# A recurrent recommendation kernel: the GRU gate matmuls split into four matmuls of 32 output columns

## The chip, the cores and the metric

The kernel runs on one core of one Trainium2 chip. The metric is the device time of one launch in microseconds (us). The kernel before takes 2076.75 us, the median of three runs between 2075.74 and 2077.31.

A core has a matrix engine (TensorE, "PE" in the profile, its weight loads apart as "PEld"), a vector engine (VectorE, "DVE"), an engine for activation functions (ScalarE, "ACT"), GpSimd ("POOL") and SyncE ("SP"), which here only issues DMAs. Each works through its own queue in order. TensorE reads SBUF and writes PSUM[...].

## The reference

For 1024 users there is a history of T = 100 item embeddings of 128 numbers. A GRU runs over the history, its states are the keys of an attention, and a second recurrence runs over the keys. All of it is f32.

```python
def gru_step(h, x_t):
    gi = x_t @ gru_Wih.T + gru_bih
    gh = h @ gru_Whh.T + gru_bhh
    i_r, i_z, i_n = jnp.split(gi, 3, axis=-1)
    h_r, h_z, h_n = jnp.split(gh, 3, axis=-1)
    r = jax.nn.sigmoid(i_r + h_r)
    z = jax.nn.sigmoid(i_z + h_z)
    n = jnp.tanh(i_n + r * h_n)
    h_new = (1.0 - z) * n + z * h
    return (h_new, h_new)
...
feat = jnp.concatenate([keys, q, keys - q, q * keys], axis=-1)
score = _mlp(feat, [(att_W0, att_b0), (att_W1, att_b1), (att_W2, att_b2)], relu)   # 512 -> 80 -> 40 -> 1
score = jnp.where(mask[:, :, None] == 1, score, -jnp.inf)
attn = jax.nn.softmax(score, axis=1)[..., 0]
pooled = jnp.einsum('bt,btd->bd', attn, keys)
```

After that, an AUGRU (a GRU whose update gate is scaled by a weight taken from `pooled`) runs over the keys, the state at each user's length is taken, and a small MLP (640 -> 200 -> 80 -> 1, sigmoid) gives one score per user.

## The kernel before, in words

Features lie on the 128 partitions, users along the free dimension. The 1024 users are two halves of HB = 512, so that a matrix product of a half is a 128 x 512 matmul and fills one PSUM bank.

The kernel has two stages. The first (`gru_phase`) runs the GRU, the attention MLP, a softmax that is kept up to date in blocks of steps, and the weighted sum of the keys ("pooled"). The second (`augru_phase`) runs the AUGRU with users sorted by length, so that its matmuls get narrower, from 510 columns to 96, and the last MLP.

The order of the instructions is written out by hand: each engine executes what concerns it in the order of the Python program. One step `s` of the loop at line 823 issues on TensorE:

- for half 0 and then half 1, the gates (`Half.gru`, line 497): r from x and h (two matmuls that accumulate in one bank), h's part of n and x's part of n (one matmul each, in banks of their own), z from x and h (two matmuls). That is six 128 x 128 x 512 matmuls for a half, twelve for a step, all issued at line 507. The pool `ps` gives their banks: six in turn.
- the attention MLP of step `s - 1` (`attend`, line 660). Its layers have 80, 40 and 1 outputs. They are packed into blocks of R = 32 outputs, and three time steps are worked on together: layer one of step s - 1, layer two of the step before, layer three of the one before that. A block is one matmul at line 669 of 32 output columns that writes 32 partitions of a bank, at the array's column position of these partitions. There are sixteen of them in a step, in four turns of four, one for each column position, into two banks of the pool `pa`.

The rest of a step lies on other engines. ScalarE takes the sigmoids and the tanh (lines 519, 538, 539) and the relu of the attention (line 708). VectorE does the GRU's elementwise work (lines 527, 537, 542 to 544), the 32 x 32 transposes of the new state (line 556), the sum of the attention result and the item's share (line 703, "f") and the product of state and item for the next attention (line 582). `stage()` puts parts of a block's softmax between the halves' work in the steps that follow a block's end; `scores` (lines 755 and 759) uses a bank of `pa` for a moment, which the attention's second result of that step needs next. GpSimd adds up the masked history (lines 493, 494) and the weighted keys (lines 605, 606). SyncE loads x and the mask two steps ahead and writes keys and scores to HBM.

Between the stages comes a tail (lines 887 to 954): the last attention turns, the last softmax blocks, a layer of the final MLP that doesn't depend on the AUGRU (line 636), and the rest of the weighted sum; then `pooled` goes through HBM to the second stage.

The wih and whh tiles hold the three gates' weights as [128, 3, 128], so that `w[:, g, :]` is a gate's 128 x 128 weight. The gate matmul is

```python
nc.tensor.matmul(
    p,
    lhsT=w[:, g, :],
    rhs=v,
    start=(j == 0),
    stop=(j == len(parts) - 1),
)
```

and the attention's is

```python
s = ts(q, R)
nc.tensor.matmul(p[i][s, :], lhsT=w[:, s], rhs=v, start=start, stop=stop)
```

In the built program every matmul carries the size of the array tile that it uses: 128 x 128 for the gates, for the item's share (line 245, once) and for the whole second stage, 128 x 32 for the attention.

## Time and profile before

| What | Value |
|---|---|
| median of the three runs | 2076.75 us |
| span of the profiled execution, first to last instruction | 2049.3 us |
| median less span | 27.4 us |
| granted TensorE clock, mean | 0.996 |
| TensorE busy | 2021.1 us, 99% |
| VectorE busy | 1756.6 us, 86% |
| GpSimd busy | 1305.1 us, 64% |
| ScalarE busy | 826.3 us, 40% |
| gate matmuls (L507), records | 1200 of x and 1188 of h |
| attention matmuls (L669), records | 3216 |
| instructions | 26686 |

The profiled execution has no time of its own beside its span; a run's time holds what lies ahead of the first and after the last instruction too.

The profile page gives the busy time of each engine, the chain of waits that ended last with its shares by line, and groups of instructions (line, engine, operation, output<-inputs, shape, count, busy time and mean duration, idle time before them and who ended it). The timeline gives single instructions or merged runs of them in order of time: start, duration, engine, line, count, and in brackets the idle time before. An f32 matmul shows as two weight loads and two matmuls. Matmuls overlap, and their ends are modelled: the distance of starts tells more than their durations. The table of windows gives each engine's busy time in a stretch. Line numbers are those of the kernel before; in the changed kernel everything below the change lies one line further down.

### The profile page before, as it was taken

How to read it: one execution, taken by the hardware profiler on the slowest of the kernel's cores; microseconds unless marked ns; L12 is line 12 of the kernel's file. 1: busy time of each engine (PE TensorE's matmuls, PEld its weight loads, DVE VectorE, ACT ScalarE, POOL GpSimd, SP SyncE). 2: the span in 40 equal slices, each digit the busy share in tenths (PEclk: the TensorE clock that was granted, in tenths of full speed). 3: DMA queues.
4: the chain of work that ended last, by engine and by line, in shares of the span. 5: the costliest groups of instructions: out<-in, count | busy, mean ns of one | idle time of the engine just before them, and what ended most of it. 6: DMA issues, size and time to landing. Idle time of an engine off the chain costs nothing.

```text
span 2049.3 us, 26686 instructions
## 1 busy us (share of the span) xinstructions
PE 2021.1 (99%) x8288; PEld 975.3 (48%) x8288; DVE 1756.6 (86%) x3066; ACT 826.3 (40%) x1508; POOL 1305.1 (64%) x1291
## 2 busy tenths in 40 slices
PE   8999999999999999999999999999899999999998
PEld 3343333333333333333333333334444556678997
DVE  6888999998989988888889898999587777888986
ACT  3334343343434343433434333434344444444554
POOL 0233939659796959597796958899753354443431
PEclk9999999999999999999999999999999999999999
DMA  4452333223334334332343233231542333333432
GB/s 118 98 115 89 104 95 105 79 85 109 112 97 114 115 98 126 108 101 84 98 124 104 91 103 104 89 104 55 169 121 87 95 111 95 94 101 93 88 80 38
DMA packets 241587, 204.73 MB, mean 100 GB/s; under 512 B 59270, under 2 KB 204394, under 8 KB 241434
## 3 DMA queue, kind: packets, MB, share of 16 engines
q1 hardware_dynamic: 227498, 170.43, 29.9%
q0 software_dynamic: 12352, 32.31, 5.7%
q8 instruction: 67, 1.10, 0.2%
q14 instruction: 86, 0.70, 0.1%
q10 hardware_dynamic: 1584, 0.20, 0.1%
HBM read 146.82 MB, written 54.40 MB: 98 GB/s over the span
## 4 chain that ended last, share of the span: by engine, by line
PE 89%; DVE 4%; DMA 2%; POOL 2%; issue 1%; ACT 1%; SPq 0%; DVEq 0%; ACTq 0%; POOLq 0%
PE ps L507 46%; PE pm L669 16%; PE ph L1075 5%; PE pr L1075 4%; PE pu L1075 4%; PE ph L1071 4%; PE pu L1071 4%; PE pr L1071 4%; DMA rows<-keys_d,idx_k 1%; DVE kq L582 1%; POOL pooled L606 1%; POOL kw L605 1%; DMA x<-in_hist_x 0%; DVE ps L537 0%; DVE d L543 0%
## 5 line engine op out<-in xcount | busy, mean ns | idle before, releaser
L507 PE MATMUL ps<-x,wih 128*128 128x512 f32 x1200 | 592.6, 603 | 4.2 <-DMA x<-in_hist_x 4.2
L507 PE MATMUL ps<-hn,whh 128*128 128x512 f32 x1188 | 574.4, 592 | 0.0
L507 PEld LDWEIGHTS ps<-x,wih 128*128 128x128 f32 x1200 | 220.9, 191 | 327.7 <-issue 252.7
L507 PEld LDWEIGHTS ps<-hn,whh 128*128 128x128 f32 x1188 | 225.7, 190 | 284.1 <-issue 275.8
L493 POOL TENSOR_TENSOR xm<-x,m 128x512 f32<-128x512 f32 x200 | 247.3, 1237 | 137.4 <-DMA m<-mask_d 137.1
L538 ACT ACTIVATE ps<-ps,bih 128x512 f32<-128x512 f32 x200 | 132.4, 662 | 484.7 <-DVE ps L537 484.7
L519 ACT ACTIVATE r<-ps,brz 128x512 f32<-128x512 f32 x200 | 137.5, 688 | 375.1 <-PE ps L507 373.9
L494 POOL TENSOR_TENSOR hist<-hist,xm 128x512 f32<-128x512 f32 x200 | 266.5, 1333 | 15.7
L174 POOL DMA_INDIRECT rows<-keys_d,idx_k x220 | 214.0, 973 | 84.9 <-POOL rows L173 70.8
L606 POOL TENSOR_TENSOR pooled<-pooled,kw 128x512 f32<-128x512 f32 x191 | 254.5, 1333 | 15.0
L605 POOL TENSOR_TENSOR kw<-kt,e 128x512 f32<-128x512 f32 x191 | 219.3, 1148 | 64.7 <-DVE e L778 64.6
L582 DVE TENSOR_TENSOR kq<-hn,item 128x512 f32<-128x512 f32 x200 | 228.3, 1181 | 0.0
L669 PE MATMUL pm<-hn,wk 128*32 128x512 f32 x1200 | 211.8, 596 | 3.3 <-ACT q L248 1.7
L669 PE MATMUL pm<-kq,wkq 128*32 128x512 f32 x1200 | 209.4, 592 | 0.0
L1083 ACT ACTIVATE c<-ph,bh 128x96 f32<-128x96 f32 (+41 forms) x198 | 96.5, 488 | 275.5 <-PE ph L1075 275.5
L669 PE MATMUL pm<-mv,w 128*32 128x512 f32 (+1 forms) x808 | 196.2, 598 | 0.9 <-DVE e L759 0.9
L703 DVE TENSOR_TENSOR f<-pm,q 128x512 f32<-128x512 f32 x200 | 128.4, 684 | 50.9 <-PE pm L669 50.7
L542 DVE TENSOR_TENSOR d<-hn,ps 128x512 f32<-128x512 f32 x198 | 136.1, 687 | 34.9 <-ACT ps L538 32.6
L543 DVE TENSOR_TENSOR d<-ps,d 128x512 f32<-128x512 f32 x200 | 138.4, 692 | 23.8 <-ACT ps L539 6.3
L537 DVE TENSOR_TENSOR ps<-ps,u 128x512 f32<-128x512 f32 x200 | 140.0, 700 | 21.2 <-PE ps L507 0.5
L173 POOL COPY rows<-rest 128x1 f32<-128x1 f32 x188 | 35.4, 188 | 191.5 <-DVE rest L1112 190.1
L527 DVE SCALAR_TENSOR_TENSOR u<-ps,bhh,r 128x512 f32<-128x512 f32 x198 | 146.9, 742 | 11.6 <-PE ps L507 11.2
(180 smaller groups left out, 2943.9 us busy)
## 6 DMA issues: line engine op xcount, KB each, us to landing
x<-in_hist_x SPq DMA_DIRECT2D x212, 256.0 KB
keys_d<-kt SPq DMA_DIRECT2D x48, 1024.0 KB
m<-mask_d SPq DMA_DIRECT2D x200, 128.0 KB
rows<-keys_d,idx_k POOLq DMA_INDIRECT x220, 3.0
s_b<-mv SPq DMA_DIRECT2D x200, 8.0 KB
keys_d<-kt SPq DMA_DIRECT2D x32, 64.0 KB
at<-att_d SPq DMA_DIRECT2D x34, 48.0 KB
mask_i<-in_mask SPq DMA_DIRECT2D x8, 200.0 KB
```

The lines of the kernel that those rows point to most:

```text
L174: nc.gpsimd.indirect_dma_start(out=r[:, at, :], out_offset=None, in_=keys_d[q], in_offset=bass.IndirectOffsetOnAxis(ap=idx_k[:, k, i : i + ...
L493: nc.gpsimd.tensor_mul(d, x, m)
L494: nc.gpsimd.tensor_add(acc, acc, d)
L507: nc.tensor.matmul(p, lhsT=w[:, g, :], rhs=v, start=(j == 0), stop=(j == len(parts) - 1),)
L527: nc.vector.scalar_tensor_tensor(out=u, in0=ph, scalar=bhh[:, 2:3], in1=r, op0=ALU.add, op1=ALU.mult,)
L537: nc.vector.tensor_add(pi, pi, u)
L582: nc.vector.tensor_mul(kq, h, item[:, self.cols])
L605: eng.tensor_mul(d, k, w)
L606: eng.tensor_add(acc, acc, d)
L669: nc.tensor.matmul(p[i][s, :], lhsT=w[:, s], rhs=v, start=start, stop=stop)
L1071: nc.tensor.matmul(p, lhsT=m[:, 1, :], rhs=k, start=True, stop=False)
L1075: nc.tensor.matmul(p, lhsT=m[:, 0, :], rhs=v, start=False, stop=True)
```

## The change

In `Half.gru`, the helper `gate` issues four matmuls where it issued one. Each takes 32 of the 128 columns of the gate's weight and writes the 32 partitions of the bank that belong to them. The moving operand (x or h, 128 x 512) is the same for the four. R is 32 and P is 128. Both parts of a gate accumulate as before, quarter by quarter.

```diff
                 def gate(g, parts):
                     p = ps.tile([P, HB], F32, tag="g", name=f"ps{g}")
                     for j, (w, v) in enumerate(parts):
-                        nc.tensor.matmul(
-                            p,
-                            lhsT=w[:, g, :],
-                            rhs=v,
-                            start=(j == 0),
-                            stop=(j == len(parts) - 1),
-                        )
+                        for q in range(P // R):
+                            nc.tensor.matmul(
+                                p[ts(q, R), :],
+                                lhsT=w[:, g, ts(q, R)],
+                                rhs=v,
+                                start=(j == 0),
+                                stop=(j == len(parts) - 1),
+                            )
                     return p
```

In the built program the gate matmuls of the changed kernel are 4776 with a tile of 128 x 32, where they were 1194 with 128 x 128. Nothing else differs but the semaphore waits and values that follow from the count.

## The prediction

> **What bounds the kernel now.** I read the page first: busy shares, the chain that ended last, the costliest groups.

> ```profile
> PE 2021.1 (99%) x8288; PEld 975.3 (48%) x8288; DVE 1756.6 (86%) x3066; ACT 826.3 (40%) x1508; POOL 1305.1 (64%) x1291
> ...
> PE ps L507 46%; PE pm L669 16%; PE ph L1075 5%; PE pr L1075 4%; PE pu L1075 4%; PE ph L1071 4%; PE pu L1071 4%; PE pr L1071 4%; DMA rows<-keys_d,idx_k 1%; DVE kq L582 1%; POOL pooled L606 1%; POOL kw L605 1%; DMA x<-in_hist_x 0%; DVE ps L537 0%; DVE d L543 0%
> ...
> L507 PE MATMUL ps<-x,wih 128*128 128x512 f32 x1200 | 592.6, 603 | 4.2 <-DMA x<-in_hist_x 4.2
> L507 PE MATMUL ps<-hn,whh 128*128 128x512 f32 x1188 | 574.4, 592 | 0.0
> ```

> The chain is TensorE for 46% + 16% of the span in the two lines of the first stage: gates (L507) and attention MLP (L669). An f32 matmul leaves two weight loads and two matmul records, so 1194 gate matmuls are 2388 records. TensorE practically never idles there. But a modelled busy time hides small gaps, so next comes its own timeline, one step of the loop (start, duration, line, count).

> ```profile
> 703.62 1.02 PE L507 MATMUL ps<-hn,whh 128*128 128x512 f32 x2
> 704.57 0.62 PE L669 MATMUL pm<-hn,wk 128*32 128x512 f32 x2
> ...
> 705.02 0.60 PE L669 MATMUL pm<-hn,wk 128*32 128x512 f32 x2
> ...
> 705.45 0.60 PE L669 MATMUL pm<-kq,wkq 128*32 128x512 f32 x2
> ...
> 707.17 1.04 PE L669 MATMUL pm<-kq,wkq 128*32 128x512 f32 x8
> 708.14 1.13 PE L507 MATMUL ps<-x,wih 128*128 128x512 f32 x2
> 709.10 1.88 PE L507 MATMUL ps<-hn,whh 128*128 128x512 f32 x4
> 710.82 1.88 PE L507 MATMUL ps<-x,wih 128*128 128x512 f32 x4
> ```

> Read the starts. The next attention starts at 718.64, so a step is 718.64 - 704.57 = 14.07 us; 93 of the 97 complete steps from 30.3 to 1399.3 us have exactly this length. Gate records follow each other every 1.72 / 4 = 0.43 us (0.4295 over a longer run). Attention records come four at a time, one per 32-column tile, and a group of four takes the same 0.43 (705.02 to 705.45). A step has 24 gate records and 32 / 4 = 8 groups: 32 slots x 0.4295 = 13.74 us. The remaining 0.33 us lies at the two changes of shape: the attention starts 0.09 late (703.62 + 0.86 = 704.48) and its first slot is 0.02 long; the gates start 0.11 late (707.17 + 0.86 = 708.03), and their first two slots take 0.96, 0.10 too many. The weight loads show the reason for the uneven parts:

> ```profile
> 704.57 0.11 PEld L669 LDWEIGHTS pm<-hn,wk 128*32 128x32 f32 x2 [0.76 <-PE ps L507]
> ...
> 708.14 0.30 PEld L507 LDWEIGHTS ps<-x,wih 128*128 128x128 f32 x2 [0.84 <-DVE hn L544]
> 708.67 0.19 PEld L507 LDWEIGHTS ps<-hn,whh 128*128 128x128 f32 x1 [0.24 <-issue]
> ```

> Inside a run, the load for the next slot begins with the present matmul. After a change the first load begins only where its own matmul is due. The releaser named at 708.14 (hn) ended at 707.97, so it is not the cause.

> Last, the windows by ten steps (us; busy time of PE, PEld, DVE, ACT, POOL) and the waits, for what stands behind TensorE.

> ```profile
> 311.70:452.40 140.70, 140.70 (x568) 54.12 (x560) 131.46 (x187) 53.11 (x85) 103.82 (x84) 1.00 0.31 93
> 733.80:874.50 140.70, 140.70 (x564) 54.12 (x560) 125.73 (x181) 54.22 (x85) 93.43 (x77) 1.00 0.39 116
> 1296.60:1437.30 140.70, 137.91 (x592) 58.34 (x584) 132.16 (x206) 54.73 (x90) 130.93 (x110) 1.00 0.29 90
> ```

> ```profile
> DVE f L703 <- PE pm L669: 50.7, 46, 3.3
> ```

> VectorE is close behind: 12.6 to 13.2 us a step. It waits for the attention result in only 46 of 100 steps.

> [...]

> **The change, part by part.**

> *Removed: the mode changes.* Gates and attention both become 128x32 tiles, so all 32 slots are of one mode: 13.74 us a step, 0.33 less, over 97 steps 32 us. The one-time matmul on the item embedding (L245) stays at 128x128 and gains one mode change, about 0.16 us; TensorE waits 1.73 us for ScalarE just after it, so I cost it at nothing (0.16 if that cover were gone). The tail between the stages keeps its changes.

> *Added: matmul instructions.* 1194 x 3 = 3582 more matmuls, so the 24 gate records of a step become 96, each with a weight load. Array time: four 32-column records per slot, as in the attention, so nothing. Weight loads: 0.11 us, beside the running matmuls, so nothing; uncovered it is the 0.02 that the attention's first slot shows, x 24 x 97 = 47 us. I take zero because the seven later attention slots show no such cost. Instruction supply: 2 x (96 + 32) = 256 instructions in 13.74 us is 53.7 ns each, against 112 in 14.07 now. No run of this kernel sustains that over whole steps. Upper bound: the late second stage (128x96, 24 instructions from 2002.56 to 2003.94) sustains 57.7 ns, and groups of four within it 56 ns[...]. Lower bound: the trace's records of TensorE's semaphore instructions[...]. In the first stage two of them with 24 matmul instructions between lie 1.02 us apart in most steps (41 ns an instruction), and two with 76 between (731.57 and 734.63) 3.06 us apart (40 ns). I take 41: 256 x 41 = 10.5 us a step, hidden under 13.74. If it is 56, the step is 14.31.

> ```profile
> 2002.56 0.39 PE L1071 MATMUL pr<-k,wr 128*128 128x96 f32 x2
> ...
> 2003.94 0.39 PE L1071 MATMUL pr<-k,wr 128*128 128x96 f32 x2
> ```

> *Added or moved waits.* In the built program each gate's semaphore wait sits on the first matmul of its four, so no wait is on a later one. The attention's first matmul waited for TensorE's own attention of the step before, long done; this wait goes, worth nothing. The state hn, which the second gate matmul of a half waits for, is ready 4 to 6 us early (707.97 against 713.83 for half 1), and no gate bank comes free less than about 4 us ahead. No DMA and no other queue moves.

> *What is late next: VectorE.* Its work in a step is its busy time plus 0.82 us of fixed gaps (0.10 + 0.18 + 0.10 + 0.03 behind ScalarE and itself, twice): 13.15 + 0.82 = 13.97 at 311 to 452 us, 13.39 at 734 to 874, 13.22 + 0.82 = 14.04 at 1297 to 1437. Against 13.74 it falls behind in the first and the last. I measured in each step how far f (L703) starts behind the step's first gate matmul: 0.14 us where VectorE is ahead, 3.7 and 3.4 at the 18th and 95th step, where now an attention matmul waits for the softmax (L759) to free a bank. Those two steps are 15.3 and 15.8 us long. Carrying this lag on (next lag = lag + VectorE's work - 13.74, not under 0.14; a softmax step with more lag than now stretches by the excess) those stretches grow from 2.9 to about 7.5 us in sum, with a new one of under 1 us near the 26th step, and the loop ends with VectorE about 0.8 us further behind: 32 - 4.6 - 0.8 = 26.6. POOL (GpSimd) competes with VectorE more densely in shorter steps (L582 takes 1181 ns where other such operations take about 690); 0.03 us a step in the roughly 30 steps where VectorE bounds is 0.9. So 25.7 us.

> *The tail.* From 1294 us POOL works back to back up to the pooled result that the second stage needs; it starts there after waiting 6 us for VectorE's weights, and later waits (1.3, 0.6, 0.9) are again for the softmax. So it moves with VectorE. The second stage is untouched.

> *Sum.* Against the profiled span: 2049.3 - 25.7 = 2023.6. The median of the runs is 27.4 us above the span; I leave that as it is: 2076.75 - 25.7 = 2051.0.

> **The rivals.** (1) The whole gain passes: VectorE's slack holds, 2076.75 - 32 = 2044.7. For it: its lag heals in most steps now. Against: the two windows with 14.0 us of work. (2) Slower: TensorE's instruction supply bounds the gate stage. It decides from 14.07 / 256 = 55.0 ns an instruction; at the 56 ns of the second stage a step is 14.31 us, + 0.24 x 97 = 24, so 2100; at 57.7, 2146. For it: nothing shown sustains 54 ns[...]. Against: 40 ns over 76. (3) The change doesn't do what it says: the 0.33 us comes with the change of operands and stays, or three more loads a slot cost the same again: 2076.

> **How the numbers follow.** Chances: forecast, VectorE takes a part, 0.60 (its own range 2047 to 2060); whole gain 0.21; no change 0.06; slower 0.13. From 0.2% (4.2 us, about what a measurement of this kernel tells from no change): faster 0.81, same 0.06, slower 0.13. The range reaches from the whole gain to the forecast's end with more contention: 2044 to 2062, leaving out 0.19.

> **What would show it.** Right: gate records at L508 in fours, 32 columns, a slot of 0.43 us, steps of 13.74 with no longer slot where lines 508 and 670 meet; longer stretches at the 18th and 95th step; fewer VectorE waits for pm. Wrong: steps above 14.07 with TensorE starts spread evenly at 56 ns or more (supply), slots of 0.45 or more (loads), or a surviving gap where the lines meet.

## The result and the profile after

The changed kernel takes 2054.97 us, the median of four runs between 2054.47 and 2055.92. The kernel before took 2077.03 us beside it (four runs, 2075.74 to 2078.45). The ratio is 0.9893, with a 95% interval of 0.9879 to 0.9907: 22.1 us less. The forecast was 2051.0, so 26.0 less than these 2077.03.

The page of the changed kernel has these lines in the places of those shown for before: busy shares, the chain that ended last, and the gate groups, whose columns are count, busy time, mean of one, and idle time ahead.

```profile
PE 1998.8 (97%) x15452; PEld 1049.1 (51%) x15452; DVE 1763.7 (86%) x3066; ACT 824.5 (40%) x1508; POOL 1313.0 (64%) x1291
...
PE ps L508 42%; PE pm L670 14%; PE ph L1076 5%; PE pr L1076 4%; PE pu L1076 4%; PE pr L1072 4%; PE pu L1072 4%; PE ph L1072 4%; DVE kq L583 1%; DMA rows<-keys_d,idx_k 1%; DVE ps L538 1%; DVE d L544 1%; DVE d L543 1%; DVE u L528 1%; ACT ps L539 1%
...
L508 PE MATMUL ps<-x,wih 128*32 128x512 f32 x4800 | 778.3, 595 | 4.6 <-DMA x<-in_hist_x 4.0
L508 PE MATMUL ps<-hn,whh 128*32 128x512 f32 x4752 | 768.1, 592 | 0.0
```

The gate records are four times as many, and each still lasts 592 to 595 ns; their busy time doesn't grow fourfold (778.3 and 768.1 us, where it was 592.6 and 574.4), because four of them overlap: four start in every 0.43 us, as the next timeline shows. The chain's shares of the two first-stage lines fall from 46% and 16% to 42% and 14%, and five of VectorE's lines now stand in it with 1% each, where only the product (kq) did.

TensorE's timeline shows the place where the two lines meet (start, duration, line, count):

```profile
697.66 1.16 PE L508 MATMUL ps<-x,wih 128*32 128x512 f32 x8
...
707.10 1.16 PE L508 MATMUL ps<-hn,whh 128*32 128x512 f32 x8
707.96 0.60 PE L670 MATMUL pm<-hn,wk 128*32 128x512 f32 x2
...
710.53 1.16 PE L670 MATMUL pm<-kq,wkq 128*32 128x512 f32 x8
711.39 1.16 PE L508 MATMUL ps<-x,wih 128*32 128x512 f32 x8
```

Eight records are two slots of four. 707.10 + 0.86 = 707.96, and 710.53 + 0.86 = 711.39: no gap at either meeting. The step is 711.39 - 697.66 = 13.73 us, where it was 14.07.

For the rest I took the start of each step `s` of the loop (its first gate matmul of x) in both traces. The prediction counted complete steps from the first attention: its 18th, 26th and 95th are s = 19, 27 and 96. From the start of s = 1 to that of s = 99 the loop takes 1364.16 us instead of 1387.02. Ninety-eight steps at the two medians, 14.068 and 13.733, differ by 32.8. Two early steps with one-time work (s = 1 and 8) are longer than the median by 5.3 before and 5.5 after. The other long steps are those in which TensorE waits for VectorE's u or for the softmax, and a few that follow on such a wait: 3.0 us in sum before (1.23 at s = 19, 1.79 at 96 and 97), 12.8 after (2.4 at s = 16 to 19, 2.4 at 27, 2.6 at 35 and 38, 5.3 at 93 to 97, and 0.1). So 32.8 - 9.8 - 0.2 = 22.8. The loop starts 0.4 earlier and the tail is 1.4 longer: the second stage starts at 1418.34 instead of 1440.28, 21.9 us earlier, which is the timed difference.

The changed kernel's profiled execution took 2054.49 us with a span of 2052.7, so a run's time is only 1.8 us above its span. The 27.4 us of before were something else: its profiled execution had a second stage of 609.0 us, while that of the changed kernel has 634.4, and both lengths come up with and without the change (last section).

### The profile page after: what moved, and what is told of

It reads as the page before. It is cut to its first block, busy times and chain, and to the rows that moved or that the text cites. A ratio compares the mean times of both kernels' runs of the same rounds, so it can differ in the third digit from the quotient of the medians.

```text
span 2052.7 us, 41040 instructions
## 1 busy us (share of the span) xinstructions
PE 1998.8 (97%) x15452; PEld 1049.1 (51%) x15452; DVE 1763.7 (86%) x3066; ACT 824.5 (40%) x1508; POOL 1313.0 (64%) x1291
## 4 chain that ended last, share of the span: by engine, by line
PE 83%; DVE 9%; issue 2%; DMA 2%; ACT 1%; POOL 1%; another core or an unknown queue 1%; SPq 0%; DVEq 0%; ACTq 0%; POOLq 0%
PE ps L508 42%; PE pm L670 14%; PE ph L1076 5%; PE pr L1076 4%; PE pu L1076 4%; PE pr L1072 4%; PE pu L1072 4%; PE ph L1072 4%; DVE kq L583 1%; DMA rows<-keys_d,idx_k 1%; DVE ps L538 1%; DVE d L544 1%; DVE d L543 1%; DVE u L528 1%; ACT ps L539 1%
## 5 line engine op out<-in xcount | busy, mean ns | idle before, releaser
L508 PE MATMUL ps<-x,wih 128*32 128x512 f32 x4800 | 778.3, 595 | 4.6 <-DMA x<-in_hist_x 4.0
L508 PE MATMUL ps<-hn,whh 128*32 128x512 f32 x4752 | 768.1, 592 | 0.0
L508 PEld LDWEIGHTS ps<-x,wih 128*32 128x32 f32 x4800 | 260.2, 110 | 291.0 <-issue 270.2
L508 PEld LDWEIGHTS ps<-hn,whh 128*32 128x32 f32 x4752 | 258.2, 110 | 280.1 <-issue 271.9
L493 POOL TENSOR_TENSOR xm<-x,m 128x512 f32<-128x512 f32 x200 | 248.1, 1240 | 121.7 <-DMA m<-mask_d 60.8
L670 PE MATMUL pm<-hn,wk 128*32 128x512 f32 x1200 | 257.1, 592 | 4.0 <-DVE f L704 2.3
L606 POOL TENSOR_TENSOR kw<-kt,e 128x512 f32<-128x512 f32 x191 | 220.1, 1153 | 62.2 <-DVE e L779 62.1
L670 PE MATMUL pm<-kq,wkq 128*32 128x512 f32 x1200 | 257.2, 592 | 0.0
L670 PE MATMUL pm<-mv,w 128*32 128x512 f32 (+1 forms) x808 | 240.5, 592 | 8.2 <-DVE e L760 8.2
L583 DVE TENSOR_TENSOR kq<-hn,item 128x512 f32<-128x512 f32 x200 | 233.0, 1204 | 0.0
L543 DVE TENSOR_TENSOR d<-hn,ps 128x512 f32<-128x512 f32 x198 | 136.1, 687 | 34.9 <-ACT ps L539 32.4
L1100 DVE TENSOR_TENSOR pu<-pu,c 128x96 f32<-128x96 f32 (+41 forms) x197 | 88.2, 448 | 86.0 <-ACT c L1084 77.4
L544 DVE TENSOR_TENSOR d<-ps,d 128x512 f32<-128x512 f32 x200 | 138.3, 691 | 22.7 <-ACT ps L540 3.4
L704 DVE TENSOR_TENSOR f<-pm,q 128x512 f32<-128x512 f32 x200 | 128.0, 681 | 26.5 <-PE pm L670 26.4
```

The lines of the kernel that those rows point to most:

```text
L493: nc.gpsimd.tensor_mul(d, x, m)
L508: nc.tensor.matmul(p[ts(q, R), :], lhsT=w[:, g, ts(q, R)], rhs=v, start=(j == 0), stop=(j == len(parts) - 1),)
L544: nc.vector.tensor_mul(d, pz, d)
L583: nc.vector.tensor_mul(kq, h, item[:, self.cols])
L606: eng.tensor_mul(d, k, w)
```

## The experiments

My theory: the whole 0.33 us a step is the price of two mode changes (changes of the tile's shape from one matmul to the next), the extra matmuls cost nothing, and what is missing from 32 us is VectorE, which has about as much work as a 13.73 us step is long. Rivals: the gain comes from the 32-column matmuls as such; TensorE's instruction supply is near its limit; a single PSUM bank or another queue, and not VectorE's work, holds back the rest. Every ratio is to the kernel before, run beside it. "The changed kernel" has line numbers as in the sections above; the experiments shift them by up to three.

**The kernel before, again**, for the relation of time and span.

> The kernel before, unchanged, to see one execution whose own time and trace belong together. The profile of before had a span 27.4 us under the median of its runs; the profile of after only 2.3 us under. Theory A: the first stage of before ends at 1440 us as in its profile, and its second stage usually takes 634 us, as in the profile of after, not the 609 us of its own profile: span about 2074, time 2076. Theory B: something outside the span costs before 27 us and after 2 us: span 2049, time 2076.

Measured: 2052.61 us (2051.36 to 2053.41), ratio 1.0001 [0.9992, 1.0010], for a span of 2051.0 in an execution of 2052.78. Neither theory holds: the distance of time and span is 1.8 us for this kernel too, and here it ran in 2052.6 us with a second stage of 609.9.

**Half 0's gates alone tiled.** The mode changes stay, two a step.

```diff
-    nc.tensor.matmul(p, lhsT=w[:, g, :], rhs=v, ...)
+    n = R if self.i == 0 else P
+    for q in range(P // n):
+        nc.tensor.matmul(p[ts(q, n), :], lhsT=w[:, g, ts(q, n)], rhs=v, ...)
```

> Only half 0's gates are issued as 32-column matmuls, half 1's stay at 128 columns. Each step still has two mode changes (half 0 to half 1, half 1 to attention). If the gain comes from the mode changes: steps of 14.06 us and 2077 us, as before. If it comes from 32-column gate matmuls being cheaper in themselves (weight load, accumulation): half of it, about 2066.

Measured: 2051.55 us (2050.35 to 2052.29), beside 2052.61; ratio 0.9995 [0.9986, 1.0004]. TensorE's timeline of one step:

```profile
706.19 1.04 PE L671 MATMUL pm<-kq,wkq 128*32 128x512 f32 x8
707.05 1.04 PE L509 MATMUL ps<-x,wih 128*32 128x512 f32 x8
...
711.34 1.04 PE L509 MATMUL ps<-hn,whh 128*32 128x512 f32 x8
712.32 1.12 PE L509 MATMUL ps<-x,wih 128*128 128x512 f32 x2
...
721.12 1.04 PE L509 MATMUL ps<-x,wih 128*32 128x512 f32 x8
```

The step is still 721.12 - 707.05 = 14.07 us. Where the attention meets the gates there is no gap any more (706.19 + 0.86 = 707.05); it lies between the halves (711.34 + 0.86 = 712.20, and the next starts at 712.32). Half of the gates in the new form bring nothing while the number of mode changes is the same. The gain doesn't come from the 32-column matmuls.

**One gate of half 0 alone tiled**, the n gate (g == 2 in the condition above). Now a step changes its mode four times.

> Only half 0's two matmuls for n (gate 2) are issued as 32-column matmuls, in the middle of gates at 128 columns: four mode changes a step, not two. If a pair of changes costs 0.33 us: steps of 14.40 us, 97 x 0.33 = 32 us more, less where VectorE set the pace already (a stall of 1 to 3 us in sum goes): about 2107. If mode changes are not what costs: 2077.

Measured: 2080.68 us (2079.90 to 2081.42), ratio 1.0142 [1.0125, 1.0159]: 28.1 us slower. Its steps are 14.40 us long, which is 14.07 + 0.33. TensorE's timeline around the tiled gate:

```profile
723.79 2.02 PE L509 MATMUL ps<-hn,whh 128*128 128x512 f32 x10
725.62 2.10 PE L509 MATMUL ps<-x,wih 128*32 128x512 f32 x10
727.56 1.02 PE L509 MATMUL ps<-hn,whh 128*128 128x512 f32 x2
```

The first two rows merge what follows on each other: two records of 128 columns and eight of 32, four slots, so 1.72 us. 723.79 + 1.72 = 725.51, but the next row starts at 725.62, 0.11 late; 725.62 + 1.72 = 727.34, but the gate after it starts at 727.56, 0.22 late. So a pair of changes costs 0.33 us in another place and with other operands as well. That it is 28 and not 32 us in all is VectorE's doing: its stretches near s = 19 and 96 (3.0 us in the trace of before, 4.0 in that of before again) are gone in the longer steps.

**The gates at 256 moving columns**, twice as many matmuls again: 448 TensorE instructions a step, where the changed kernel has 256.

```diff
-    for j, (w, v) in enumerate(parts):
-        for q in range(P // R):
-            nc.tensor.matmul(p[ts(q, R), :], ..., rhs=v, ...)
+    for c in range(2):
+        for j, (w, v) in enumerate(parts):
+            for q in range(P // R):
+                nc.tensor.matmul(p[ts(q, R), ts(c, HB // 2)], ..., rhs=v[:, ts(c, HB // 2)], ...)
```

> All gate matmuls of 32 columns and, besides, 256 moving columns instead of 512: twice the gate instructions, 448 matmul instructions and weight loads a step, the same array work. It measures how many instructions TensorE's sequencer supplies. At 41 ns each, as the distances of its semaphore instructions in the trace of before say: steps of 448 x 41 = 18.4 us, about 2510 us. At 54 ns: 24.2 us a step, 3070 us. If supply is no limit down to 30 ns: steps of 13.7 to 14.1 and about 2055 to 2090.

Measured: 2039.14 us (2037.15 to 2040.14) beside 2052.61; ratio 0.9935 [0.9918, 0.9952]. The row of windows for ten steps (length; busy time and count of PE, PEld, DVE, ACT, POOL):

```profile
841.52:979.46 137.94, 137.94 (x2246) 79.26 (x2242) 123.66 (x182) 55.04 (x86) 95.67 (x78) 1.00 0.38 115
```

2246 + 2242 instructions in 137.94 us are 30.7 ns each, and the step is 13.79, only 0.06 longer than with 256. The rival that lets supply decide from 55 ns is far off: the changed kernel asks for one every 53.7 ns, and for it the supply has room to spare. Whether 30.7 ns is itself a limit was not tried; counted by matmuls alone it is 137.94 / 2246 = 61.4 ns. (The kernel gains 8.6 us less than the changed kernel does, 13.5 against 22.1. Of that, 0.06 x 98 = 6 lie in the steps. VectorE's stretches are as long as in the changed kernel, 12.9 and 12.8 us in sum, but s = 8 exceeds the median by 6.2 us instead of 1.7: TensorE idles 2.48 us there, for something that the trace doesn't name. That this one gap is of supply is not excluded.)

**VectorE's product left out**, in the kernel before and in the changed one. The attention takes the state itself in place of the product of state and item, so this feature is not computed. VectorE loses two operations a step, some 2.4 us, and no matmul waits for the product any more; nothing else changes.

```diff
-    kq = wp.tile([P, HB], F32, name="kq")
-    nc.vector.tensor_mul(kq, h, item[:, self.cols])
-    self.first = h, kq
+    self.first = h, h
```

The kernel before without it:

> The kernel before without the product of state and item (the attention MLP gets the state in the product's place, so its features differ): 2.4 us a step less for VectorE, all else equal. TensorE bounds its steps at 14.07 us in both theories; the three longer steps (1.3, 1.2 and 1.7 us) lose up to 3 us, the tail perhaps 1 to 4: 3 to 7 us below the kernel before.

The changed kernel without it:

> The changed kernel without the same product. If VectorE (and the softmax bank it releases late) took the rest of the gain: all steps are 13.73 us, no long ones at the softmax, and the first stage is 97 x 0.34 = 33 us shorter than that of before_no_kq, perhaps 2 less where GpSimd bounds the tail. If something else took it (instruction fetch, weight loads): the difference stays 22 us and the long steps stay.

The changed kernel as it is, beside them:

> The changed kernel, unchanged, beside the kernel before on a chip where before may take 2052 or 2077. Its profile had a second stage of 634 us where three other kernels had 609 to 610. If the 25 us belong to the change (its first stage leaves something late for the second): 2055 again, with a second stage of 634 us. If they belong to the circumstances of that comparison, in which before took 2077 too: whatever before takes, 22 us less, so 2030 beside 2052.

Measured, beside 2079.59 us for before:

| kernel | us | ratio, 95% interval |
|---|---|---|
| before, product left out | 2072.41 | 0.9969 [0.9958, 0.9979] |
| changed, product left out | 2040.56 | 0.9810 [0.9794, 0.9827] |
| changed | 2059.97 | 0.9906 [0.9889, 0.9922] |

Without the product the change brings 2072.41 - 2040.56 = 31.9 us, all that the mode changes cost; with it 19.6. In the trace the loop takes 1350.22 instead of 1383.00 us, 32.8 less, and no step but the two early ones is above 13.73. Twenty steps in a row are, in the row of windows of the changed kernel without the product, 274.66 / 20 = 13.73 us each:

```profile
688.77:963.43 274.66, 274.66 (x2564) 149.33 (x2560) 205.92 (x315) 109.40 (x169) 196.71 (x167) 1.00 0.36 108
```

So the missing 10 to 12 us were VectorE's work, directly or through what it sets off. The run takes away the product's share of work and its meetings with GpSimd at once, and doesn't tell these two apart.

**The softmax's transpose in a gate's bank.** The most visible stalls are attention matmuls that wait for the bank which the softmax (L756, L760) holds. Is it the bank?

```diff
-    pt = pa.tile([P, KH, R], F32, tag="a", name="pt")
+    pt = ps.tile([P, KH, R], F32, tag="g", name="pt")
```

> The changed kernel with the softmax's transposed scores in a bank of the gates' pool instead of the attention's pool. The matmuls that stand still at the softmax (in the profile of after 0.9, 2.1, 1.7, 1.1, 0.2, 1.9 and 0.3 us, 8 in sum) no longer wait for VectorE to release that bank. If these waits are what TensorE loses for good: 5 to 8 us faster than the changed kernel. If VectorE's total work is what bounds: 0 to 3 us, as the wait moves to another matmul. A gate may in turn wait for the bank: up to 3 us slower.

Measured: 2062.79 us (2059.49 to 2064.63), ratio 0.9916 [0.9899, 0.9933], against 0.9906 [0.9889, 0.9922] for the changed kernel in the same session: not faster. The waits went to the gates; TensorE's timeline at s = 27, with the idle time before and its releaser in brackets:

```profile
385.45 1.06 PE L508 MATMUL ps<-x,wih 128*32 128x512 f32 x8 [0.98 <-DVE u L528]
388.53 1.94 PE L508 MATMUL ps<-x,wih 128*32 128x512 f32 x8 [2.01 <-DVE d L544]
```

A gate now finds its bank still in VectorE's hands. The steps but for the early two exceed 13.73 by 21 us in sum, where the changed kernel beside it has 14; the mean granted clock is 0.989 in this execution and 0.990 in the changed kernel's, so by my estimate (0.001 x 2063) some 2 of these 7 us can be the clock's. The run takes a bank from the gates for a moment instead of adding one to the kernel's pools of six and two, so it shows only that the wait goes along with whatever VectorE holds. That VectorE's work makes the backlog is shown by the run without the product and by the next two.

**Half 1's product on GpSimd**, in the first 40 steps and in the first 88. This does the whole computation. VectorE loses one operation a step, GpSimd gains one.

```diff
-    nc.vector.tensor_mul(kq, h, item[:, self.cols])
+    eng = nc.gpsimd if self.i and t < 40 else nc.vector
+    eng.tensor_mul(kq, h, item[:, self.cols])
```

The first 40:

> The changed kernel with half 1's product of state and item on GpSimd instead of VectorE for the first 40 steps; the whole computation is done. If VectorE's work per step is what holds back the rest of the gain, the stalls of TensorE before the 14th to 35th steps (0.49, 0.86, 2.07, 1.72 us and the longer steps 15 to 18) go: some 6 us less than the changed kernel in the same session. Rival: GpSimd's and VectorE's operations on SBUF slow each other down, and GpSimd's product comes late for the attention: no gain, or slower by up to some us.

The first 88:

> The same for the first 88 steps. If VectorE's work is the only limit, the same 6 us less, and 1 or 2 us more since VectorE enters the last stretch (92nd to 96th step) as far ahead as it can be. If GpSimd's queue is what is late next, its weighted sum falls behind in the later steps and the tail before the second stage gets longer by what it falls behind: each product is some 1.2 us of GpSimd, which has 13.7 x 0.25 = 3 us a step to spare, so not before the last 10 steps.

The changed kernel beside them:

> The changed kernel as it is, beside the two: 20 to 23 us less than before.

Measured, beside 2077.93 us for before:

| kernel | us | ratio, 95% interval |
|---|---|---|
| product of half 1 on GpSimd, 40 steps | 2048.50 | 0.9855 [0.9839, 0.9872] |
| the same, 88 steps | 2048.30 | 0.9856 [0.9839, 0.9872] |
| changed | 2055.89 | 0.9892 [0.9875, 0.9908] |

They are 7.4 and 7.6 us below the changed kernel: they beat both kernels. Up to s = 40 every step after the early two is 13.73. What is left is s = 93 to 96 (4.8 us with 40 steps, 4.4 with 88) and, with 40 alone, 1.0 at s = 49 and 51, which the times can't tell. The 1 or 2 us more that I expected of 88 steps didn't come: with 88 steps VectorE's f starts 0.39 us behind its step at s = 89, and 5.33 behind at s = 96, as in the changed kernel (5.32). The rival was that the two engines slow each other down so much that nothing is gained. The times speak against it, and so do the windows. Here are those of s = 10 to 19, the product alone, first of the changed kernel (VectorE), then of the 40-step one (VectorE, GpSimd):

```profile
140.90:280.62 139.72, 20.67 (x20) 1.00 0.29 89
```

```profile
141.16:278.49 137.33, 7.59 (x10) 12.86 (x10) 1.00 0.30 90
```

The half that VectorE keeps takes 759 ns instead of 1034, so VectorE saves 13.1 us of 20.7 with half of the operations gone; GpSimd needs 1286 ns for each of its own.

**A ninth buffer for x.** In the changed kernel one of the stalls, at s = 35, has another look than the rest. SyncE's queue and VectorE's timeline there:

```profile
497.72 0.33 SPq L477 DMA_DIRECT2D x<-in_hist_x  x1
498.10 0.42 SPq L482 DMA_DIRECT2D m<-mask_d  x1
498.62 1.15 SPq L716 DMA_DIRECT2D s_b<-mv  x2
```

```profile
500.90 0.73 DVE L756 STREAM_TRANSPOSE pt<-s_b 128x512 f32<-128x512 f32 x1 [2.17 <-DMA s_b<-mv]
```

ScalarE had the scores (mv) ready at 493.5, but their DMA starts at 498.62. It stands behind a load of x that begins at 497.72, and that is the moment when GpSimd's reading of an old x ends (L493, 496.53 + 1.17 = 497.70). GpSimd works back to back there, so its work lies later in a shorter step: the load starts 8.7 us into the step, where it was 5.4 before. Nine buffers instead of eight leave every engine's order as it is.

```diff
-    x = xp.tile([P, HB], F32, name="x")
+    x = xp.tile([P, HB], F32, name="x", bufs=9)
     ...  # and bufs=9 likewise at the five other tiles that use these buffers
```

> The changed kernel with nine buffers for x instead of eight; nothing else, and the order of the instructions on every engine is the same. In the changed kernel's trace VectorE's transpose of the scores at the 36th step waits 2.17 us for the scores' DMA, which stands in SyncE's queue behind a load of x that waits for GpSimd to free a buffer. If that is the cause of the stall there, TensorE's gap of 1.72 us at that step goes, the gaps of 0.86 and 2.07 us at the 20th and 28th step, where VectorE works back to back, stay, and the time is some 1 to 3 us below the changed kernel's, so a ratio of 0.987 to 0.990. If VectorE's backlog alone makes all three, all three stay and so does the time (ratio 0.989 to 0.9905). The gaps decide, since the time is near what the measurement can tell.

Measured: 2052.33 us (2050.88 to 2055.26), ratio 0.9881 [0.9865, 0.9898]; the time alone can't tell this from the changed kernel. The gaps do. SyncE and VectorE at the same place:

```profile
494.82 1.12 SPq L716 DMA_DIRECT2D s_b<-mv  x2
499.44 0.34 SPq L477 DMA_DIRECT2D x<-in_hist_x  x1
```

```profile
500.36 0.72 DVE L756 STREAM_TRANSPOSE pt<-s_b 128x512 f32<-128x512 f32 x1
```

The scores leave at once, the wait of 2.17 is gone, and so is TensorE's gap of 1.72; s = 35 to 38 exceed 13.73 by 0.1 us in sum instead of 2.6. The gaps of 0.86 at s = 19 and 2.08 at s = 27 are there as before. So there are two causes, and both start with engines whose work doesn't shrink with the step. (With half 1's product on GpSimd the stall at s = 35 was gone as well: GpSimd's order is another there, and the scores leave ahead of the load.)

## Why the prediction was right, and where its sizes were off

*The mode changes: right.* 0.33 us a step was read from one step of the profile, and the runs confirm the price: the pair moved (14.07), removed (13.73), one more added (14.40).

*Array time, loads and supply: right for this change.* The slots are 0.43 us, and no load shows. The 41 ns an instruction was my estimate, from the distances of semaphore instructions in the trace of before, and 55.0 the point from which the rival decides; 30.7 ns has been sustained, so those distances were not the least that supply allows. That the 56 to 57.7 ns of the second stage are no limit of supply was not shown by the trace of before; the 30.7 ns show it. And the 0.02 us that the prediction takes for an uncovered load isn't the length of one: the load records last 110 ns for 32 columns and 190 for 128. Only the difference, 80 ns, is that of the 0.02 and 0.10 us by which the first slots after a change are too long.

*L245's mode change: not seen.* The step that holds it (s = 1) exceeds the median by 3.8 us, where it was 4.0; but in three other traces of the changed kernel's kind it is 3.9 to 4.6, so that a term of 0.16 can't be told there.

*VectorE: right in kind, under-sized.* The prediction let the stretches grow from 2.9 to 7.5 us and took 0.8 for the end of the loop and 0.9 for contention, 6.3 in all. Measured: the stretches grow by 9.8 and the tail by 1.4. At s = 27 I expected under 1 us. VectorE's timeline there has no gap, and TensorE's shows who pays:

```profile
388.51 0.69 DVE L545 TENSOR_TENSOR hn<-ps,d 128x512 f32<-128x512 f32 x1
389.12 0.72 DVE L756 STREAM_TRANSPOSE pt<-s_b 128x512 f32<-128x512 f32 x1
389.87 0.29 DVE L760 TENSOR_TENSOR e<-pt,on 128x128 f32<-128x128 f32 x1
```

```profile
390.30 0.59 PE L670 MATMUL pm<-mv,w 128*32 128x512 f32 x1 [2.07 <-DVE e L760]
```

The two stretches that the prediction carried on, around s = 19 and 96, come to 2.4 + 5.3 = 7.7 us; its 7.5, less the new one of under 1, left more than 6.5 for them, so they were nearly right. What was missed is s = 27 (2.4 instead of under 1), s = 35 and 38 (2.6 instead of nothing, the load of x below) and part of the tail.

At s = 27 it is the lag and not contention. The rows of windows for s = 20 to 27, first before, then after (VectorE is the third busy time):

```profile
286.09:398.64 112.55, 112.55 (x450) 43.30 (x449) 105.22 (x152) 42.08 (x67) 84.10 (x69) 1.00 0.33 99
```

```profile
280.62:392.91 112.29, 110.22 (x1029) 40.54 (x1025) 105.36 (x151) 42.25 (x68) 85.44 (x69) 1.00 0.33 100
```

VectorE's work is the same. With the fixed gaps it is 105.36 / 8 + 0.82 = 13.99 us a step, 0.26 more than 13.73, and eight such steps make 2.1 us of lag, near the 2.4. The prediction had the work right, 13.97: its own 13.97 - 13.74 = 0.23 a step makes 1.8 in eight steps, so the under 1 us doesn't follow from the figures that it gives.

Contention (that the product takes longer beside GpSimd's work, see the last section), "0.03 us a step", was too small as well, but it fell where it cost little. In the whole program VectorE's busy time grew by 7.1 us where I had put 0.9. About half of it lies in s = 36 to 43, first before, then after:

```profile
511.20:623.75 112.55, 112.55 (x453) 43.30 (x449) 99.42 (x141) 42.33 (x67) 99.40 (x81) 1.00 0.35 102
```

```profile
504.67:615.25 110.58, 110.58 (x1030) 53.45 (x1026) 103.24 (x143) 42.08 (x68) 97.53 (x79) 1.00 0.35 105
```

Of these 3.8 us, 2.2 are the product (L583), which takes 1278 ns there instead of 1142; two more operations fall into the second window. TensorE lost 0.7 us in these steps, at s = 38, and nothing in the same steps of the run with nine buffers. How much of the tail and of the last stretch is contention was not tried.

The lag model also knew one place of collision only, the softmax. At s = 16 to 18 gates wait for a bank that VectorE's u (L528) frees (the gaps are 0.49 and 0.18 us; the steps exceed 13.73 by 1.3). The prediction's sentence "no gate bank comes free less than about 4 us ahead" held for before only: it was checked with VectorE's lag of then. The table of waits shows the lost slack (total, times, longest): VectorE waits 26.4 us for the attention result, in 28 steps, where it was 50.7 in 46, and TensorE now waits 8.2 us for the softmax, where it was 0.9:

```profile
DVE f L704 <- PE pm L670: 26.4, 28, 3.3
...
PE pm L670 <- DVE e L760: 8.2, 7, 2.1
```

*"No DMA and no other queue moves": wrong, 2.6 us.* The instructions keep their order, but GpSimd's back-to-back work moves against the shorter step, and with it SyncE's load of x and the scores' DMA behind it.

*The tail: right in kind*, it moved with VectorE (it is 1 to 3 us shorter in both kernels without the product), and lost 1.4 us where 0.8 was forecast. *The median's 27.4 us above the span: a wrong reading*, though without consequence, since I left it as a common offset.

*The rivals.* The whole gain is what comes when VectorE has 2.4 us less to do (31.9). The slower case fell with the changed kernel's own steps and the 256-column run. That the change doesn't do what it says fell with the timeline.

## What to carry to other kernels

Look for alternating tile shapes in TensorE's timeline by the distance of starts, not by busy time: the 0.33 us of a pair was invisible in "99% busy", and splitting the wide matmuls into the narrow form removed it at no cost in array time (slots of 0.43 us before and after). Before counting on such a gain, add up every other engine's work per step against the new step: one at 13.4 to 14.0 of 13.73 us gave back a third here. A fixed order of instructions is no protection, for an engine that works back to back drifts against a shorter step (here a load that waits for GpSimd started 8.7 us into a step instead of 5.4), and buffers and queues that were free in time can stop being so; moving one operation to an engine with slack (7.5 us here), or one more buffer (here it removed a stall, but its gain in time is within what can be told), is then the next step.

## What the hardware showed beyond expectation

A short gap can cost more than itself. At s = 27 TensorE idles 2.07 or 2.08 us in every run of the changed kernel's kind, but the step exceeds 13.73 by 2.4 us in one trace and by 4.2 in three others. The windows right after the gap, first of the changed kernel (2.4), then of the one with nine buffers (4.2):

```profile
390.30:393.34 3.04, 3.04 (x30) 1.13 (x33) 2.65 (x5) 1.24 (x2) 1.59 (x2) 1.00 0.03 5
```

```profile
390.41:393.60 3.19, 3.19 (x17) 1.03 (x21) 2.80 (x5) 1.24 (x2) 1.65 (x2) 0.54 0.02 5
```

The first column after the engines is the granted clock: 1.00 in the first, 0.54 in the second, where slots take 0.85 us instead of 0.43. The same work after the gap, up to the next gate, takes 392.91 - 390.30 = 2.61 us in the first and 394.71 - 390.41 = 4.30 in the second, 1.7 more, nearly the 1.8 between the two steps. So a gap of 2 us cost 2 to 4. Why the clock was lower after one of two gaps of the same length, the traces don't show.

VectorE's product of two f32 operands from SBUF takes 675 to 1773 ns in the changed kernel between 141 and 281 us, while its operations with an operand in PSUM take 682 to 742 in the mean. The spread goes with GpSimd's work. Of the 200 products of the whole trace, the 49 beside which GpSimd runs no elementwise operation take 671 to 684 ns; the 117 that take more than 820 ns all have at least 742 ns of such work beside them; the other 34 have some too and take no more than 812. Why, the trace doesn't show. Moving work to GpSimd helped here all the same, since VectorE was the limit and its other product got faster as well (759 ns instead of 1034).

The second stage's length differs by 25 us between sessions, whatever the kernel: 609 to 610 us in the profiles of before, of before again, of half 0 tiled, of one gate tiled and of the 256-column kernel, 634 to 638 in those of the changed kernel and, with its gates as before, of the one without the product. In the longer form TensorE waits once, 12 us in the changed kernel's trace, for VectorE's first state, and VectorE itself waits for something that the trace doesn't name:

```profile
1457.33 0.70 DVE L1021 TENSOR_TENSOR spare<-spare,first_u 128x512 f32<-128x512 f32 x1 [9.80 <-remote]
```

That accounts for about half. No trace of the kernel before itself in the longer form was kept; that its 2077 us hold it is read from the time. The changed kernel didn't bring it: run again beside the kernel before, it took 2059.97 where that took 2079.59. All experiments with the short form ran on one chip, and those with the long form on three others; whether the chip makes it, or something else that differed, was not tried, and the cause stays open. The ratios aren't touched, since each is taken against the kernel before in the same session.
